# C times the states on GpSimd for 14 of 16 groups, five state buffers, silu in place, the odd heads' k by chunk

## The chip, the cores and the metric

The kernel runs on one core of a Trainium2 chip. A core has a matrix engine (TensorE, PE in the profile), a vector engine (VectorE, DVE), an engine for activation functions (ScalarE, ACT), a programmable engine (GpSimd, POOL) and a queue engine (SyncE, SP) that starts transfers. Each takes its instructions in a fixed order from its own queue, and semaphores hold an instruction back until what it needs is there. The metric is the device time of one execution in microseconds; lower is better.

## The reference

The input x is 16 sequences of 512 tokens with 256 features. Four blocks follow one another, each with a layer norm in front and a residual sum behind it: a state-space block, a gated feed-forward block with 4-bit quantization, a linear attention, and the same feed-forward block again with the same weights.

```python
x = x + mamba(layernorm(x));   x = x + ffn(layernorm(x))
x = x + linattn(layernorm(x)); x = x + ffn(layernorm(x))
# mamba, for every token t: 256 channels d, 16 states n
dA  = dt[t, d] * A[d, n]
h   = exp(dA) * h + (sum_d(dA * u[t, d]) * B[t, n])     # the added term is the same for all d
y   = sum_n(h[d, n] * C[t, n]) + Dp[d] * u[t, d]
# ffn: q() quantizes blocks of 16 to a 4-bit grid times a scale
ffn = q(silu(q(x) @ q(w_gate).T) * (q(x) @ q(w_up).T)) @ q(w_down).T
# linattn: 16 heads of 16, feature map elu + 1 on q and k, causal running sums
y   = (q . cumsum(k v)) / (q . cumsum(k) + 1e-6)
```

## The kernel before

All numbers are fp32, except the rounding operand of the quantizer (bf16). Tiles have 128 partitions.

The state-space block of one sequence (`mamba`) has 256 channels times 16 states, that is 4096 rows of 512 tokens. A tile holds 128 rows (16 states of 8 channels) twice, side by side: a group of 128x1024. There are 16 groups per sequence (`steps`: two halves e, four j, two q0). For each, SyncE spreads the channels' dt over the partitions (`spread`, a transfer from DRAM), ScalarE makes the decays exp(dt A) (`decay`, L466 and L469, into one of two `bars`), VectorE runs the recurrence as a scan along time (L485) into a state buffer `h`, and VectorE multiplies the states by C, in place (L489); C is one row tile `cm` used for both halves. When two groups are done, TensorE adds the rows of a channel with four matmuls into the bank `py` (L495). There are three state buffers (tag "hs"). After the last group of a half, ScalarE copies `py` out (L500).

The feed-forward block (`ffn`) quantizes the normed x (`fp4_steps`: a maximum per block, L212; half and its reciprocal, L217 and L219; the division, L226; on ScalarE the rounding operand, L230; two rounding steps, L232 and L233; the product with the scale, L234). Then, chunk by chunk of 128 tokens and half by half of 704 hidden features, TensorE makes gate and up (L535), ScalarE the tanh of half the gate into `sg` (L541), and VectorE (tanh + 1) times gate (L542) and times half of up (L545) into `h`. The chunk is quantized by the same steps, transposed, and multiplied by the down weights (L574). Names end in _f for the first and in _g for the second feed-forward block.

The attention makes q and k as features by tokens (L607 to L615), multiplies k by a mask that keeps the odd heads (`ko`, one ScalarE instruction on 128x1024 per sequence, L624), and then works by chunk: scores (L653), the causal mask (L660), the values, and the running sum of k v. The denominator is put in shape by a GpSimd copy `dx` (L694) of 128x256, transposed by TensorE (L699) and used on VectorE (L704). `kt` (L710) is the chunk's k by tokens.

The layer norm (`layernorm`) takes statistics on VectorE (L356 to L359), the power -0.5 on GpSimd (`rstd`, 128x4, L361) and normalizes on VectorE (`xn`, L364). The rstd of the four norms and the dx copies are what GpSimd does after the start.

Order: the program is written as generators that yield weights, in units meant as microseconds. `by_turns` always advances the half whose share of its given total is smallest, `weave` alternates pieces of two. For sequence b, first come its state-space block and the beginning of its first feed-forward block, up to a total FIRST, beside the second feed-forward block of sequence b-2 and the norm of the attention of b-1 (FRONT + FFN2); then the rest of that feed-forward block (CHUNKS) beside the attention (ATTN). A group of `mamba` yields 3.5. The compiler's scheduler then orders each engine's queue from this: the earlier written goes first among what it expects to be ready, so engines' orders differ from the written one (two scans can stand next to each other before the first one's multiplication).

```python
FIRST, CHUNKS, FRONT, ATTN, FFN2 = 80.0, 30.0, 7.85, 23.0, 42.0
halves = [(some(new, FIRST), FIRST)]
halves.append((weave(last_ffn(b - 2), some(at, FRONT), 0), FRONT + FFN2))
by_turns(halves)
by_turns([(new, CHUNKS), (at, ATTN if b > 1 else FRONT + ATTN)])
```

Of the kernel before, what the change touches and what calls it, by code (L numbers as in the profile page):

```python
# [10 lines left out]
F32 = mybir.dt.float32  # L11
# [21 lines left out]
def kernel(  # L33
# [411 lines left out]
    def mamba(b, xt):  # L445
# [29 lines left out]
        for at, (e, j, q0) in enumerate(steps):  # L475
            bar = ahead
            if at + NSP - 1 < len(steps):
                sps.append(spread(*steps[at + NSP - 1]))
            if at + 1 < len(steps):
                ahead = decay(sps[at + 1], *steps[at + 1])  # L480
            if j == 0 and q0 == 0:
                py = ps_y.tile([P, S], F32, tag="y", name=f"py_{b}_{e}")
                nc.tensor.matmul(py, d_diag[:, e], u[:, e, :], start=True, stop=False)
            h = one.tile([P, 2, S], F32, tag="hs", name=f"h_{b}_{e}_{j}_{q0}", bufs=3)
            nc.vector.tensor_tensor_scan(  # L485
                h.rearrange("p i t -> p (i t)"), bar.rearrange("p i t -> p (i t)"),
                inp.rearrange("p i t -> p (i t)"), 0.0, ALU.mult, ALU.add,
            )
            nc.vector.tensor_tensor(h, h, cm.unsqueeze(1).to_broadcast([P, 2, S]), ALU.mult)  # L489
            if q0 == 0:  # L490
                h0 = h
            else:

                for q in range(4):
                    nc.tensor.matmul(  # L495
                        py[32 * q : 32 * q + 32, :], red[:, j, :], (h0, h)[q // 2][:, q % 2, :],
                        start=False, stop=(j == 3),
                    )
            if j == 3 and q0 == 2:
                nc.scalar.copy(yT[:, e, :], py)  # L500
            yield 3.5


        for c in range(0, NC, 2):
# [12 lines left out]
    def ffn(i, nm, xt):  # L517
# [8 lines left out]
        def hidden(c):  # L526

            h = act.tile([P, FF], F32, tag="h", name=f"h_{nm}_{c}", bufs=2)
            for f in range(2):
# [3 lines left out]
                for pw, wT in ((pg, wgT), (pu, wuT)):  # L533
# [3 lines left out]
                            start=(k == 0), stop=(k == ND - 1),  # L537
                        )

                sg = act.tile([P, HF], F32, tag="sg", name=f"sg_{nm}_{c}_{f}", bufs=2)  # L540
                nc.scalar.activation(sg, pg[:, :HF], AF.Tanh, scale=0.5)  # L541
                nc.vector.scalar_tensor_tensor(  # L542
                    sg, sg, 1.0, pg[:, :HF], ALU.add, ALU.mult
                )
                nc.vector.scalar_tensor_tensor(  # L545
                    h[:, cols], sg, 0.5, pu[:, :HF], ALU.mult, ALU.mult
                )
                yield 1
            fp4(act, h, FF, f"{nm}_{c}")
            hs.append(h)  # L550
# [42 lines left out]
    def attention(b, xt):  # L593
# [25 lines left out]
            qk.append(ft)  # L619
        qf, kf = qk  # L620


        ko = att.tile([P, ND, S], F32, tag="ko", name=f"ko_{b}", bufs=1)
        nc.scalar.activation(ko, kf, AF.Copy, scale=odd_heads[:, 0:1])  # L624
        yield 0.1

        def scores(c):

            tok = ts(c, P)
# [15 lines left out]
            )  # L645
            yield 0.1

            psc = [bank(f"psc_{b}_{c}_{g}") for g in range(4)]
            for s in range(NH // 4):
                e, odd = divmod(s, 2)  # L650
                for g in range(4):
                    rows = slice(32 * g, 32 * g + (2 * HD if odd else HD))
                    nc.tensor.matmul(  # L653
                        psc[g][:, ts(s, P)], (ko if odd else kf)[rows, e, tok],
                        qf[rows, e, tok], start=True, stop=True,
                    )
            sm = []
# [12 lines left out]
        def attend(c, vp, sm):  # L670
# [19 lines left out]
            num = att.tile([P, ND, P], F32, tag="num", name=f"num_{b}_{c}")  # L690
            nc.scalar.copy(num, pn)

            dx = att.tile([P, ND * HB, HD], F32, tag="dx", name=f"dx_{b}_{c}")
            nc.gpsimd.tensor_copy(  # L694
                dx, den[:, c * NH : (c + 1) * NH].unsqueeze(2).to_broadcast([P, NH, HD])
            )
# [8 lines left out]
            if c < NC - 1:  # L705
                pk = bank(f"pk_{b}_{c}")
                for e in range(ND):
                    nc.tensor.transpose(pk[:, ts(e, P)], kf[:, e, tok], ident)
                kt = att.tile([P, D], F32, tag="kt", name=f"kt_{b}_{c}")
                nc.scalar.copy(kt, pk[:, :D])  # L710
                pkv = bank(f"pkv_{b}_{c}")[:, :D].rearrange("p (e t) -> p e t", t=P)
                if c > 0:
# [82 lines left out]

    FIRST, CHUNKS, FRONT, ATTN, FFN2 = 80.0, 30.0, 7.85, 23.0, 42.0

    def some(gen, total):  # L800

# [74 lines left out]
```

## Time and profile before

| | |
|---|---|
| median of 3 runs | 2910.93 us (2910.67 to 2912.76) |
| the profiled execution's own time | 2910.69 us |
| its span, first to last instruction | 2908.9 us |
| granted TensorE clock, mean | 0.915 |
| scans L485, DVE | 256 of 2277 ns |
| multiplications by C L489, DVE | 256 of 1213 ns |
| rstd L361, POOL | 64; median 1006 to 1912 ns by norm |
| dx copies L694, POOL | 64; median 400 ns |
| ko L624, ACT | 16 of 1149 ns |

A group's line in the profile has its place, engine, operation, operands with shapes, number, then busy time, mean duration of one, and the engine's idle time before them with what ended it. A timeline line has start, length, engine, place and operands. VectorE starts an instruction some 0.08 us before the recorded end of the one in front, so durations add up to slightly more than the busy time. One sequence takes about 173 us in the steady part; the last 275 us, after the last sequence's scans, hold feed-forward and attention alone.

### The profile page before, as it was taken

The numbers are of one execution on the slowest core, as the hardware profiler recorded it, in microseconds if no ns is written. First come the engines' busy times: TensorE is split into PE (matmuls) and PEld (weight loads), VectorE is DVE, ScalarE is ACT, GpSimd is POOL, SyncE is SP. The second block draws the span as 40 slices with busy tenths as digits, with TensorE's granted clock in tenths as the row PEclk, the third lists the DMA queues.
The fourth block names the chain that finished last, engine by engine and source line by source line (L and its number), as shares of the span: only waits on it lengthen the run. The fifth ranks groups of instructions, "written<-read, shape, count | busy, mean of one in ns | idle before, by whom it ended". The sixth has DMA issues, their size and how long they took to land.

```text
span 2908.9 us, 33292 instructions
## 1 busy us (share of the span) xinstructions
PE 2441.2 (84%) x12639; PEld 1428.2 (49%) x12639; DVE 2545.1 (87%) x3795; ACT 1349.0 (46%) x2286; POOL 121.1 (4%) x153
## 2 busy tenths in 40 slices
PE   5676888888888988888888888888888888887887
PEld 2233545454554545455454545545455454545555
DVE  7897889989899898989989898998989999898565
ACT  5555454454545445453545445444544544542122
POOL 2000000000000000000000000000000000000000
PEclk8787899998998999899999999999999899989898
DMA  5332112031321313122031321303122130310000
GB/s 159 87 80 73 51 44 80 15 95 44 80 59 29 81 29 86 53 61 63 21 88 44 80 58 44 80 15 95 44 80 59 36 81 22 84 47 8 1 1 15
DMA packets 64372, 165.21 MB, mean 57 GB/s; under 512 B 8434, under 2 KB 26836, under 8 KB 64212
## 3 DMA queue, kind: packets, MB, share of 16 engines
q1 hardware_dynamic: 62592, 162.03, 21.4%
q8 instruction: 99, 1.62, 0.2%
q10 hardware_dynamic: 1620, 1.06, 0.1%
q14 instruction: 61, 0.50, 0.1%
HBM read 146.28 MB, written 16.78 MB: 56 GB/s over the span
## 4 chain that ended last, share of the span: by engine, by line
DVE 55%; PE 29%; ACT 7%; issue 5%; POOL 2%; POOLq 0%; DVEq 0%; ACTq 0%
DVE h L485 16%; DVE h L489 7%; PE pqk L607 3%; DVE sm L660 2%; PE po_g L574 2%; PE pg_f L535 2%; PE pu_f L535 2%; PE pg_g L535 2%; DVE amax_f L212 2%; PE pu_g L535 2%; PE pz L396 2%; PE py L495 2%; DVE h_f L234 1%; DVE v_f L232 1%; DVE v_f L226 1%
## 5 line engine op out<-in xcount | busy, mean ns | idle before, releaser
L485 DVE TENSOR_TENSOR_SCAN h<-bar,inp 128x1024 f32<-128x1024 f32 x256 | 578.1, 2277 | 10.1 <-ACT inp L441 8.9
L466 ACT ACTIVATE bar<-sp,a_col 128x511 f32<-128x511 f32 x512 | 348.7, 715 | 411.3 <-DVE h L485 410.8
L495 PE MATMUL py<-h,red 128*32 128x512 f32 x1024 | 271.4, 684 | 89.1 <-DVE h L489 89.1
L489 DVE TENSOR_TENSOR h<-h,cm 128x1024 f32<-128x1024 f32 x256 | 309.2, 1213 | 0.0
L469 ACT ACTIVATE bar<-bar 128x1022 f32<-128x1022 f32 x256 | 269.8, 1054 | 4.5
L574 PE MATMUL po_g<-wdT,hqT_g 128*128 128x256 f32 (+1 forms) x768 | 199.8, 403 | 33.1 <-ACT hqT_g L565 33.1
L574 PE MATMUL po_f<-wdT,hqT_f 128*128 128x256 f32 (+1 forms) x768 | 204.7, 410 | 7.8 <-ACT hqT_f L565 7.7
L535 PE MATMUL pg_f<-wgT,tT_f 128*128 128x352 f32 x512 | 200.5, 517 | 2.5 <-DVE sm L660 2.2
L535 PE MATMUL pu_f<-wuT,tT_f 128*128 128x352 f32 x512 | 180.0, 475 | 14.4 <-DVE sm L660 14.4
L574 PEld LDWEIGHTS po_f<-wdT,hqT_f 128*128 128x128 f32 (+1 forms) x768 | 141.4, 197 | 96.3 <-issue 26.8
L574 PEld LDWEIGHTS po_g<-wdT,hqT_g 128*128 128x128 f32 (+1 forms) x768 | 138.3, 193 | 94.3 <-ACT hqT_g L565 47.2
L535 PE MATMUL pg_g<-wgT,tT_g 128*128 128x352 f32 x512 | 178.4, 471 | 0.0
L535 PE MATMUL pu_g<-wuT,tT_g 128*128 128x352 f32 x512 | 173.5, 461 | 0.0
L660 DVE TENSOR_TENSOR sm<-psc,causal 128x512 f32<-128x512 f32 x256 | 163.5, 680 | 9.9 <-PE psc L653 7.9
L230 ACT ACTIVATE big_f<-v_f 128x704 bf16<-128x704 f32 (+1 forms) x80 | 67.3, 841 | 203.2 <-DVE v_f L226 203.0
L535 PEld LDWEIGHTS pu_f<-wuT,tT_f 128*128 128x128 f32 x512 | 100.9, 199 | 79.1 <-DVE sm L660 21.7
L607 PE MATMUL pqk<-tT_a,w_qkv_sb 128*128 128x512 f32 x256 | 135.6, 670 | 0.7 <-ACT tT_a L377 0.7
L535 PEld LDWEIGHTS pg_g<-wgT,tT_g 128*128 128x128 f32 x512 | 97.8, 195 | 74.9 <-issue 37.1
L535 PEld LDWEIGHTS pg_f<-wgT,tT_f 128*128 128x128 f32 x512 | 94.7, 205 | 70.5 <-issue 17.7
L535 PEld LDWEIGHTS pu_g<-wuT,tT_g 128*128 128x128 f32 x512 | 98.1, 192 | 55.1 <-issue 1.5
L495 PEld LDWEIGHTS py<-h,red 128*32 128x32 f32 x1024 | 36.4, 114 | 176.8 <-DVE h L489 118.0
L541 ACT ACTIVATE sg_g<-pg_g 128x352 f32<-128x352 f32 x128 | 58.8, 459 | 108.2 <-PE pg_g L535 108.0
(224 smaller groups left out, 4483.8 us busy)
## 6 DMA issues: line engine op xcount, KB each, us to landing
sp<-dd SPq DMA_DIRECT2D x256, 512.0 KB, 4.6
x<-in_L_attn_a_x_dram SPq DMA_DIRECT2D x16, 512.0 KB, 4.7
dd<-dt SPq DMA_DIRECT2D x128, 64.0 KB, 1.7
out_dram<-x SPq DMA_DIRECT2D x16, 512.0 KB, 3.0
w_qkv_sb<-in_L_attn_b_W_attn_dram ACTq DMA_DIRECT2D x1, 768.0 KB, 6.8
raw_d<-in_L_ffn_w_down_dram SPq DMA_DIRECT2D x1, 704.0 KB
raw_g<-in_L_ffn_w_gate_dram SPq DMA_DIRECT2D x1, 640.0 KB, 6.4
raw_u<-in_L_ffn_w_up_dram SPq DMA_DIRECT2D x1, 640.0 KB, 6.2
```

Source lines behind the costliest of these rows:

```text
L212: nc.vector.tensor_reduce(amax, src.rearrange("p (b k) -> p b k", k=BLK), AX.X, ALU.max, apply_absolute_value=True,)
L230: nc.scalar.activation(big, v, AF.Abs, scale=STEP)
L466: nc.scalar.activation(bar[:, i, 1:S], sp[:, i, 1:S], AF.Exp, scale=a_col[:, g : g + 1])
L469: nc.scalar.activation(bar[:, :, 1:S], bar[:, :, 1:S], AF.Square)
L485: nc.vector.tensor_tensor_scan(h.rearrange("p i t -> p (i t)"), bar.rearrange("p i t -> p (i t)"), inp.rearrange("p i t -> p (i t)"), 0.0, ...
L489: nc.vector.tensor_tensor(h, h, cm.unsqueeze(1).to_broadcast([P, 2, S]), ALU.mult)
L495: nc.tensor.matmul(py[32 * q : 32 * q + 32, :], red[:, j, :], (h0, h)[q // 2][:, q % 2, :], start=False, stop=(j == 3),)
L535: nc.tensor.matmul(pw[:, :HF], xqT[:, k, ts(c, P)], wT[:, k, cols], start=(k == 0), stop=(k == ND - 1),)
L541: nc.scalar.activation(sg, pg[:, :HF], AF.Tanh, scale=0.5)
L574: nc.tensor.matmul(po[:, :D], hqT[:rows, r, :], wdT[:rows, r, :], start=(r == 0), stop=(r == NR - 1),)
L607: nc.tensor.matmul(pz, w_qkv_sb[:, k, ts(je, P)], xnT[:, k, :], start=(k == 0), stop=(k == ND - 1),)
L660: nc.vector.tensor_tensor(t, psc[g].rearrange("p (s t) -> p s t", t=P), causal.unsqueeze(1).to_broadcast([P, NH // 4, P]), ALU.mult,)
```

## The change

The multiplication of the states by C moves from VectorE to GpSimd for the groups 0 to 13 of each sequence; groups 14 and 15 keep VectorE. There are five state buffers instead of three. In the feed-forward block the tanh is written straight into the hidden tile `h`, and both products are made there in place; the tiles `sg` go. `ko` is made per chunk (128x256, two buffers) inside `scores`, instead of once per sequence (128x1024). `dx` and `kt` have one buffer instead of two. The weights of the interleaving are changed: 2.3 instead of 3.5 for a group, FIRST 61 instead of 80, FRONT 7.8 instead of 7.85, and the yield behind the old `ko` goes.

```diff
-            h = one.tile([P, 2, S], F32, tag="hs", name=f"h_{b}_{e}_{j}_{q0}", bufs=3)
+            h = one.tile([P, 2, S], F32, tag="hs", name=f"h_{b}_{e}_{j}_{q0}", bufs=5)
...
-            nc.vector.tensor_tensor(h, h, cm.unsqueeze(1).to_broadcast([P, 2, S]), ALU.mult)
+            by = nc.vector if at >= len(steps) - 2 else nc.gpsimd
+            by.tensor_tensor(h, h, cm.unsqueeze(1).to_broadcast([P, 2, S]), ALU.mult)
...
-            yield 3.5
+            yield 2.3
...
-                sg = act.tile([P, HF], F32, tag="sg", name=f"sg_{nm}_{c}_{f}", bufs=2)
-                nc.scalar.activation(sg, pg[:, :HF], AF.Tanh, scale=0.5)
-                nc.vector.scalar_tensor_tensor(
-                    sg, sg, 1.0, pg[:, :HF], ALU.add, ALU.mult
-                )
-                nc.vector.scalar_tensor_tensor(
-                    h[:, cols], sg, 0.5, pu[:, :HF], ALU.mult, ALU.mult
-                )
+                hc = h[:, cols]
+                nc.scalar.activation(hc, pg[:, :HF], AF.Tanh, scale=0.5)
+                nc.vector.scalar_tensor_tensor(hc, hc, 1.0, pg[:, :HF], ALU.add, ALU.mult)
+                nc.vector.scalar_tensor_tensor(hc, hc, 0.5, pu[:, :HF], ALU.mult, ALU.mult)
...
-        ko = att.tile([P, ND, S], F32, tag="ko", name=f"ko_{b}", bufs=1)
-        nc.scalar.activation(ko, kf, AF.Copy, scale=odd_heads[:, 0:1])
-        yield 0.1
...
+            ko = att.tile([P, ND, P], F32, tag="ko", name=f"ko_{b}_{c}")
+            nc.scalar.activation(ko, kf[:, :, tok], AF.Copy, scale=odd_heads[:, 0:1])
...
-                        psc[g][:, ts(s, P)], (ko if odd else kf)[rows, e, tok],
+                        psc[g][:, ts(s, P)], ko[rows, e, :] if odd else kf[rows, e, tok],
...
-            dx = att.tile([P, ND * HB, HD], F32, tag="dx", name=f"dx_{b}_{c}")
+            dx = att.tile([P, ND * HB, HD], F32, tag="dx", name=f"dx_{b}_{c}", bufs=1)
...
-                kt = att.tile([P, D], F32, tag="kt", name=f"kt_{b}_{c}")
+                kt = att.tile([P, D], F32, tag="kt", name=f"kt_{b}_{c}", bufs=1)
...
-    FIRST, CHUNKS, FRONT, ATTN, FFN2 = 80.0, 30.0, 7.85, 23.0, 42.0
+    FIRST, CHUNKS, FRONT, ATTN, FFN2 = 61.0, 30.0, 7.8, 23.0, 42.0
```

## The prediction

> **What bounds the kernel now.** I read first the page's busy table and its chain, then the groups of instructions, then windows of one sequence, then the few places where GpSimd and VectorE already work at the same time.
>
> ```profile
> span 2908.9 us, 33292 instructions
> PE 2441.2 (84%) x12639; PEld 1428.2 (49%) x12639; DVE 2545.1 (87%) x3795; ACT 1349.0 (46%) x2286; POOL 121.1 (4%) x153
> DVE 55%; PE 29%; ACT 7%; issue 5%; POOL 2%; POOLq 0%; DVEq 0%; ACTq 0%
> L485 DVE TENSOR_TENSOR_SCAN h<-bar,inp 128x1024 f32<-128x1024 f32 x256 | 578.1, 2277 | 10.1 <-ACT inp L441 8.9
> L489 DVE TENSOR_TENSOR h<-h,cm 128x1024 f32<-128x1024 f32 x256 | 309.2, 1213 | 0.0
> 953.10:1082.00 128.90, 111.52 (x666) 66.65 (x664) 121.72 (x176) 60.24 (x104) 5.46 (x7) 0.93 0.20 54
> 1082.00:1126.00 44.00, 37.88 (x123) 20.84 (x123) 34.88 (x60) 22.91 (x37) 1.01 (x1) 0.92 0.29 72
> ```
>
> VectorE (DVE) is the fullest engine and carries 55% of the chain; TensorE (PE) is close behind with 29%. GpSimd (POOL) is almost empty. The two window lines (window, length, then busy us of PE, PEld, DVE, ACT, POOL, then clock, DMA share, GB/s) split one period of about 173 us: in the first 129 us lie all 16 scans of a sequence, and DVE is busy for 121.7 of them, PE for 111.5.
>
> Does POOL work run freely beside DVE? The next lines are from the views of lines L694 and L361 (min/median/max) and the timelines of DVE and POOL.
>
> ```profile
> L694 POOL COPY dx<-den x64: 396/400/2394, 288.2 to 2816.3; 128x256 f32<-128x256 f32 x64
> L361 POOL TENSOR_TENSOR rstd_a<-var_a,neg_half x16: 1006/1912/1913, 221.3 to 2756.4; 128x4 f32<-128x4 f32 x16
> ...
> 288.64 2.48 DVE L485 TENSOR_TENSOR_SCAN h<-bar,inp 128x1024 f32<-128x1024 f32 x1
> 288.19 3.12 POOL L694 COPY dx<-den 128x256 f32<-128x256 f32 x2 [59.18 <-DVE den L760]
> 2699.59 1.10 DVE L226 TENSOR_TENSOR v_f<-h_f,inv_f 128x704 f32<-128x704 f32 x1
> 2699.22 0.74 POOL L694 COPY dx<-den 128x256 f32<-128x256 f32 x2 [51.10 <-DVE half_f L217]
> 876.44 1.22 DVE L232 SCALAR_TENSOR_TENSOR v_g<-big_g,v_g 128x1024 f32<-128x1024 bf16 x1
> 876.62 1.91 POOL L361 TENSOR_TENSOR rstd_a<-var_a,neg_half 128x4 f32<-128x4 f32 x1 [8.78 <-DVE var_a L359]
> ```
>
> It does not. Two copies that need 0.40 each took 3.12 around a scan, the second ending at 291.31, 0.19 after the scan (291.12). The scan took 2.48 instead of 2.28, and the multiplication at 2699.59 took 1.10 instead of its mean 0.89, so POOL holds DVE up too. The rstd at 876.62 took 1.91 instead of 1.01: it ends 0.87 after L232. All these DVE instructions read two tensors from SBUF. Beside L542 and L545, which read one from SBUF and one from PSUM, the copy keeps its 0.40. So I call "exclusive" a DVE instruction with two SBUF tensors: the scans L485, the multiplication L489, the quantizer's L226, L232, L233, L234, and L615, L747, L416, L430, L750. One of those and a reading POOL instruction run one after the other. The rest ("free": L212, L542, L545, L660, L356, L364, L578 and so on) overlaps with POOL.
>
> The Trainium skill states the same in SBUF — State Buffer, Who interferes with whom: a VectorE instruction with two SBUF inputs and a GpSimd instruction that reads SBUF block each other for a whole instruction, and whichever starts first wins. It speaks against this change more strongly than the sum below: with no cover at all, every moved multiplication would cost DVE its whole length, and the time would go up.
>
> **The change part by part.**
>
> Removed from DVE: 14 x 16 = 224 of the L489 multiplications. One lasts 1.213 and the next starts 0.08 before its end (835.00 + 1.21 against 836.13), so each frees 1.13: **-254 us** of DVE.
>
> Added to POOL: 224 multiplications of 128x1024 by a broadcast row. No row has one. Lower bound: one element per step at the slope of the memsets, (524 - 204) ns / (512 - 128) = 0.83 ns, so 0.95 us with start. Upper bound: the whole 0.40 of a 256-element copy for each quarter and each of two inputs, 3.2 us. (The pow at 5437 ns for 32 elements is another kind of operation.) Nearest: what a copy adds to an exclusive DVE instruction, 0.20 to 0.21 for 256 elements of one input; eight times that is 1.6 to 1.7, and with the copy's remaining 0.2 about 1.8 to 1.9. A second stream through the same port may cost some more: I take **2.0 us**. POOL is then busy 28 us of a 173 us period, far from a bound itself.
>
> The Trainium skill, GPSIMD Engine Reference, Elementwise — side-by-side cycle accounting, gives 4497 ns for a two-input add of 2048 elements, which I estimate as 2.25 us here. By that figure the stall below would be 1.05 instead of 0.90, 236 us in total, and the sum -8 instead of -43: no gain worth the name. No run here shows it yet.
>
> The stall on DVE. For each of the 224 scans I went along DVE's recorded order behind it, without the L489s; an exclusive instruction at the head is let through first (77 of 224 cases: POOL waits for it), and then free instructions and idle time are added up to the next exclusive one. That is what POOL can hide behind. At 2.0 us a mean of 1.10 is hidden and 0.90 stalls: **+201 us**. At 0.95 it is 0.31 (70 us), at 1.75 0.74 (167), at 2.6 1.27 (285), at 3.2 1.65 (370). Break-even is at 2.3. In all, DVE's timeline of the 129 us window adds up to 44.6 us of free work and 7.2 us idle against 28 us of POOL, so the cover exists; it only lies badly.
>
> POOL's queue: the multiplications now stand in front of rstd (L361, four per sequence, three of them in the scan window) and dx (L694). xn (L364) on DVE waits for rstd, already 44 us in all. POOL is taken 28/129 = 22% of the window, for 1.0 more on average: 48 x 0.22 x 1.0 = **+10 us**; at the worst 48 x 2.0 = 96. dx feeds transposes of PE whose product L704 is read on DVE; one POOL length late is hidden by PE's other work, else 0.22 x 64 x 1.0 = 14.
>
> PE's matmuls L495 now wait for POOL. A pair of groups is ready 2 to 5 us later, and PE's in-order queue waits with it (L495 waited 89 us for L489 so far). Five state buffers instead of three let two more scans run on meanwhile; scans are some 8 us apart on average, so I count nothing; without that cover 2 us for each of 112 pairs, 224.
>
> Yields 3.5 to 2.3, FIRST 80 to 61, FRONT 7.85 to 7.8: the scan groups keep 36.8/61 = 60% of the first part's weight instead of 56/80 = 70%. The other half of that part, 49.85 units, then advances by 1.88 units per group instead of 2.18: about a seventh less work between scans. Taken as nothing, since the hidden 1.10 is mostly bounded by the next exclusive instruction; at the worst a seventh of it, 0.16 x 224 = 35.
>
> Silu in place: the same three instructions, so no work changes. tanh on ACT now waits for the readers (transposes, L561) of the h buffer two chunks back, where L545 waited for them before, and the decays L466 and L469 stand behind it on ACT. L545's whole idle time is 19 us, mostly for PE's pu; that is also the bound. Taken 0.
>
> ko by chunk: 64 copies of 128x256 by the like row L691 (364 ns), 23.3 us, for 18.4 us in 16 (L624): +5 us on ACT, which is 46% busy; 0, at worst 5. kt and dx with one buffer: kt waits for the pkv matmuls of the chunk before, a whole chunk earlier: 0. dx waits for the transposes of the chunk before, in POOL's queue, with multiplications behind it (a rival below).
>
> Sum on DVE: -254 + 201 + 10 = -43. DVE carries 55% of the chain and PE, at 111.5 of 128.9 us in the window, does not get shorter; I let 0.6 of a DVE gain reach the end: -25. The profiled execution took 2910.69 (1.8 outside its span), the median is 2910.93, so the two are one number: **2885 us**. Under 0.2% (6 us) nothing can be told from no change.
>
> **The rivals.**
>
> A, the forecast: half of a POOL multiplication hides. With stalls of 0.7 to 1.0 (157 to 224 us) the sum is -87 to -20, of which 0.6 arrives: 2859 to 2899.
>
> B, the port decides against it: the instruction behind a scan is exclusive more often, or POOL takes more than 2.3. For it: 77 cases already begin so, and two scans often stand back to back (L485 x2). If only 0.55 of 2.0 hides, the stall is 1.45 x 224 = 325 and the sum -254 + 325 + 10 = +81: 2992. Against it: the 44.6 us of free work. It decides from a stall of 1.09 per multiplication on, and a DVE loss goes to the end undiminished.
>
> C, cover is good: POOL at 1.6 or free work moved behind the scans. Stall 0.31, 70 us: -174, of which 0.6 arrives: 2806. PE's 111.5 of 128.9 is the floor, about 17 us per period.
>
> D, POOL's queue: dx already waits for PE's transposes 157.6 us in 32 cases, 4.9 each. With one buffer multiplications stand behind that; if half of it reaches the scans, 79 us more than the forecast: about 2964. Against it: five state buffers and that most of these waits are early arrivals.
>
> E, the freed DVE time becomes waiting for PE, or stall equals saving: within 6 us of 2911.
>
> **How the numbers follow.** A 0.37, C 0.15, E 0.08, B 0.33, D 0.07. Faster by over 0.2%: 0.52; within: 0.08; slower: 0.40. The 80% range goes from C's 2806, rounded down, to just short of B's 2992: 2800 to 2985. A alone has 2859 to 2899.
>
> **What would show it.** L489 on POOL with a spacing of about 2.0 when undisturbed; durations of the scans and of L226 to L234 raised by 0.9 x 224 = 201 us altogether, while L542, L545, L660 and L212 stay as they are; DVE busy by the page about 2545 - 254 + 201 = 2490; idle before xn up by 10; L495 waiting for POOL instead of DVE. The forecast is wrong if POOL needs over 2.3, if exclusive instructions gather behind the scans, or if idle before L364 or L495 grows by tens of us.

## The result and the profile after

The changed kernel takes **3144.44 us** (median; 3143.98 to 3145.93) against 2911.04 us for the kernel before on the same chip: a ratio of **1.080** with a 95% interval of 1.078 to 1.082. It is 233 us slower. The forecast was 2885 with a range up to 2985, so the time lies outside the range, on the side of rival B (the port decides) and well beyond the price of that rival. The profiled execution took 3145.93 us, 1.7 more than its span.

The page of the kernel after, with the lines that answer to those shown of before (busy time of each engine, shares of the chain, the groups of C times the states and of the scans, the dx copies):

```profile
span 3144.2 us, 33577 instructions
PE 2510.8 (80%) x12639; PEld 1477.6 (47%) x12639; DVE 2550.9 (81%) x3571; ACT 1358.4 (43%) x2334; POOL 794.0 (25%) x377
DVE 48%; PE 26%; issue 7%; POOL 6%; ACT 5%; DMA 1%; SPq 0%; POOLq 0%; ACTq 0%; DVEq 0%
L491 POOL TENSOR_TENSOR h<-h,cm 128x1024 f32<-128x1024 f32 x224 | 661.4, 2961 | 1159.0 <-DVE h L485 1098.7
L485 DVE TENSOR_TENSOR_SCAN h<-bar,inp 128x1024 f32<-128x1024 f32 x256 | 722.1, 2835 | 54.3 <-ACT bar L469 41.3
L690 POOL COPY dx<-den 128x256 f32<-128x256 f32 x64 | 36.4, 568 | 381.1 <-PE pr L695 199.5
```

VectorE has 224 instructions fewer (3795 to 3571) and is busy for 2550.9 us, where it was busy for 2545.1. So 254 us of multiplications went away, and the busy time is still 6 us up because other instructions became longer: the scans alone grew from 578.1 to 722.1 us. Worse, nearly the whole loss of time stands outside the busy time: span minus busy is 593 us on VectorE, and was 364. TensorE shows the like, 2510.8 of 3144.2 us busy against 2441.2 of 2908.9; it has the same 12639 matmuls, at a lower granted clock (0.864 instead of 0.915). Neither engine was given more work; both wait more.

The view of windows, one period of the steady part (window, length, busy us of PE, PEld, DVE, ACT, POOL, TensorE's clock, DMA share, GB/s): the first line from the first scan of a sequence to the end of its last, the second the rest.

```profile
1031.80:1144.20 112.40, 89.06 (x558) 52.47 (x556) 97.42 (x119) 46.65 (x79) 43.52 (x19) 0.83 0.24 62
1144.20:1219.50 75.30, 64.70 (x231) 38.50 (x231) 59.14 (x104) 37.29 (x65) 4.00 (x3) 0.93 0.16 40
```

The period grew from 172.9 to 187.7 us. The scans now lie closer together, in 112 us instead of 129, but the rest of the period grew from 44 to 75 us: work that used to stand between the scans has been pushed behind them. In the scan window VectorE is busy for 87% of the time (94% before) and TensorE is granted 0.83 of its clock (0.93 before).

By "the port" is meant below whatever makes a GpSimd instruction that reads SBUF and a VectorE instruction such as a scan wait for each other. How it is shared is seen in the timelines of VectorE and GpSimd in that window (start, length, engine, place, operands, and in brackets the idle time in front).

```profile
1092.56 1.73 DVE L217 TENSOR_SCALAR half_f<-amax_f 128x44 f32<-128x44 f32 x1
1106.03 4.42 DVE L485 TENSOR_TENSOR_SCAN h<-bar,inp 128x1024 f32<-128x1024 f32 x1
1112.23 2.90 DVE L485 TENSOR_TENSOR_SCAN h<-bar,inp 128x1024 f32<-128x1024 f32 x1 [1.71 <-ACT bar L469]
1115.82 3.98 DVE L485 TENSOR_TENSOR_SCAN h<-bar,inp 128x1024 f32<-128x1024 f32 x1
...
1091.89 2.35 POOL L491 TENSOR_TENSOR h<-h,cm 128x1024 f32<-128x1024 f32 x1 [2.30 <-DVE h L485]
1105.94 2.36 POOL L491 TENSOR_TENSOR h<-h,cm 128x1024 f32<-128x1024 f32 x1 [11.35 <-DVE h L485]
1110.62 2.37 POOL L491 TENSOR_TENSOR h<-h,cm 128x1024 f32<-128x1024 f32 x1 [2.32 <-DVE mv_g L357]
1115.30 2.35 POOL L491 TENSOR_TENSOR h<-h,cm 128x1024 f32<-128x1024 f32 x1 [2.31 <-DVE h L485]
1119.94 2.36 POOL L491 TENSOR_TENSOR h<-h,cm 128x1024 f32<-128x1024 f32 x1 [2.30 <-DVE h L485]
```

The multiplication that starts on GpSimd at 1105.94 ends at 1108.30. The scan that starts 0.09 us after it ends at 1110.45, that is 2.15 after the multiplication: it waited and then took its own time, and shows 4.42 us instead of 2.28. Only then does GpSimd get its next turn (1110.62), so multiplications follow each other every 4.6 to 4.7 us. The stalled scan has a second effect. There are two buffers of decays, and a scan that ends late frees its one late: by the chain of waits ScalarE starts on the next one at 1110.53, 0.08 after the scan's end, and the scan at 1112.23 stands idle for 1.71 us until that `bar` is there. And the small L217 at 1092.56, a tensor_scalar that needs 0.18 us alone, ends 0.05 us after GpSimd's multiplication (1094.24) and takes 1.73.

The waits of VectorE, summed over the span (what it waited for, us in total, times, longest), the kernel after:

```profile
DVE qk L613 <- ACT ep L612: 138.7, 30, 6.8
DVE x L576 <- PE po_g L572: 77.7, 19, 6.2
DVE x L734 <- PE pro L730: 51.9, 34, 3.0
DVE h L485 <- ACT bar L469: 41.3, 29, 10.2
DVE xn_m L364 <- POOL rstd_m L361: 35.3, 13, 2.9
```

Before, the same five stood at 25, 16, 28, under 2 and 12.5 us; three of them as the view of before has them:

```profile
DVE qk L615 <- ACT ep L614: 25.3, 29, 1.6
DVE x L578 <- PE po_g L574: 16.1, 6, 6.2
DVE xn_m L364 <- POOL rstd_m L361: 12.5, 13, 1.0
```

None of them alone explains the 229 us of added idle time; the experiments have to say which part of the change brings which.

### The profile page after: what moved, and what is told of

Read it like the earlier page. It is cut to its first block, busy times and chain, and to the rows that moved or that the text cites. A ratio compares the mean times of both kernels' runs of the same rounds, so it can differ in the third digit from the quotient of the medians.

```text
span 3144.2 us, 33577 instructions
## 1 busy us (share of the span) xinstructions
PE 2510.8 (80%) x12639; PEld 1477.6 (47%) x12639; DVE 2550.9 (81%) x3571; ACT 1358.4 (43%) x2334; POOL 794.0 (25%) x377
## 4 chain that ended last, share of the span: by engine, by line
DVE 48%; PE 26%; issue 7%; POOL 6%; ACT 5%; DMA 1%; SPq 0%; POOLq 0%; ACTq 0%; DVEq 0%
DVE h L485 14%; POOL h L491 4%; PE py L497 3%; PE po_g L572 3%; PE pu_f L537 2%; PE pqk L605 2%; PE pg_f L537 2%; DVE v_g L232 2%; DVE sm L656 2%; DVE amax_f L212 2%; DVE amax_g L212 2%; DVE v_g L226 2%; DVE half_f L217 2%; DVE v_f L226 1%; DVE v_g L233 1%
## 5 line engine op out<-in xcount | busy, mean ns | idle before, releaser
L491 POOL TENSOR_TENSOR h<-h,cm 128x1024 f32<-128x1024 f32 x224 | 661.4, 2961 | 1159.0 <-DVE h L485 1098.7
L485 DVE TENSOR_TENSOR_SCAN h<-bar,inp 128x1024 f32<-128x1024 f32 x256 | 722.1, 2835 | 54.3 <-ACT bar L469 41.3
L537 PE MATMUL pg_f<-wgT,tT_f 128*128 128x352 f32 x512 | 215.5, 550 | 68.1 <-DVE sm L656 34.3
L572 PE MATMUL po_g<-wdT,hqT_g 128*128 128x256 f32 (+1 forms) x768 | 221.9, 437 | 46.5 <-ACT hqT_g L563 46.5
L537 PE MATMUL pu_f<-wuT,tT_f 128*128 128x352 f32 x512 | 199.3, 517 | 30.1 <-DVE sm L656 30.1
L572 PEld LDWEIGHTS po_g<-wdT,hqT_g 128*128 128x128 f32 (+1 forms) x768 | 154.1, 214 | 124.2 <-ACT hqT_g L563 60.5
L656 DVE TENSOR_TENSOR sm<-psc,causal 128x512 f32<-128x512 f32 x256 | 162.3, 676 | 20.1 <-PE pn L680 10.9
L361 POOL TENSOR_TENSOR rstd_f<-var_f,neg_half 128x4 f32<-128x4 f32 x16 | 16.1, 1007 | 577.9 <-DVE var_f L359 577.9
L537 PEld LDWEIGHTS pu_f<-wuT,tT_f 128*128 128x128 f32 x512 | 110.5, 219 | 106.3 <-DVE sm L656 43.2
L613 DVE SCALAR_TENSOR_TENSOR qk<-ep 128x512 f32<-128x512 f32 x64 | 46.2, 721 | 138.7 <-ACT ep L612 138.7
L690 POOL COPY dx<-den 128x256 f32<-128x256 f32 x64 | 36.4, 568 | 381.1 <-PE pr L695 199.5
```

Of the source, the lines that this page charges most:

```text
L485: nc.vector.tensor_tensor_scan(h.rearrange("p i t -> p (i t)"), bar.rearrange("p i t -> p (i t)"), inp.rearrange("p i t -> p (i t)"), 0.0, ...
L491: by.tensor_tensor(h, h, cm.unsqueeze(1).to_broadcast([P, 2, S]), ALU.mult)
L537: nc.tensor.matmul(pw[:, :HF], xqT[:, k, ts(c, P)], wT[:, k, cols], start=(k == 0), stop=(k == ND - 1),)
L572: nc.tensor.matmul(po[:, :D], hqT[:rows, r, :], wdT[:rows, r, :], start=(r == 0), stop=(r == NR - 1),)
L656: nc.vector.tensor_tensor(t, psc[g].rearrange("p (s t) -> p s t", t=P), causal.unsqueeze(1).to_broadcast([P, NH // 4, P]), ALU.mult,)
```

## The experiments

**Stall** below is the time by which VectorE's instructions last longer than the median of their form in the kernel before, summed where the excess is over 0.05 us; it is 1 us before and **248 us** after. "Idle" is the span minus VectorE's busy time. The kernel before runs at 2911 to 2913 us beside all of these. Each expectation names the theories as they stood when it was written.

### All of the change but GpSimd, and GpSimd alone

e1: the change with every multiplication on VectorE.

```diff
-            by = nc.vector if at >= len(steps) - 2 else nc.gpsimd
+            by = nc.vector
```

> The changed kernel with all 16 multiplications by C back on VectorE; five state buffers, silu in place, ko by chunk, single dx and kt and the new weights stay. Theory 1 (port: a GpSimd multiplication and a VectorE instruction that reads two SBUF tensors exclude each other, 2.36 us each time) and theory 2 (lateness: what costs is that C times h comes later, and TensorE waits) both expect the loss to go: 2880 to 2940 us, scans back at 2.28 us each, half-clock time of TensorE back near 499 us. Theory 3 (weights: the new weights 2.3, 61 and 7.8 bunch the scans and leave VectorE without work later) expects at least half of the loss of 233 us to stay: over 3030 us. Theory 4 (the small edits: one dx buffer, one kt buffer, tanh into h) expects over 3030 us as well.

e2: the kernel before with these two lines alone changed (three buffers, old weights, no other edit).

```diff
-            nc.vector.tensor_tensor(h, h, cm.unsqueeze(1).to_broadcast([P, 2, S]), ALU.mult)
+            by = nc.vector if at >= len(steps) - 2 else nc.gpsimd
+            by.tensor_tensor(h, h, cm.unsqueeze(1).to_broadcast([P, 2, S]), ALU.mult)
```

> The kernel before with nothing changed but the multiplication by C on GpSimd for groups 0 to 13: three state buffers, old weights, old silu, ko, dx and kt. Theories 1 and 2 expect the whole loss or more, since three buffers give less room: 3100 to 3250 us. Theories 3 and 4 expect less than a third of it: under 2990 us.

Measured: e1 2975.35 us, ratio 1.022 [1.020, 1.023]; e2 3187.58, ratio 1.094 [1.093, 1.096]. e2 has a stall of 279 us and an idle time of 600. So the move to GpSimd is by itself a loss larger than the whole change, and the rest of the change is a loss too, of 64 us, which the forecast had at nothing. From e1 to the full change are 169 us: VectorE's busy time grows by 25 (2526 to 2551) and its idle time by 144 (449 to 593). In the waits of e1 the places that GpSimd lengthens can be told from those that were long without it:

```profile
DVE x L576 <- PE po_g L572: 20.6, 6, 6.2
DVE xn_m L364 <- POOL rstd_m L361: 11.6, 13, 0.9
```

With GpSimd these two are 77.7 and 35.3 us (the wait before the like `po_f` falls, from 48.6 to 20.2), and the wait for the decays goes from nothing to 41.3; the largest one, before `qk`, is 132.8 us in e1 already.

### The weights

e3: the change with the old weights. e5: the kernel before with the new ones. e6: e1 with the old ones.

```diff
-            yield 2.3
+            yield 3.5
...
-    FIRST, CHUNKS, FRONT, ATTN, FFN2 = 61.0, 30.0, 7.8, 23.0, 42.0
+    FIRST, CHUNKS, FRONT, ATTN, FFN2 = 80.0, 30.0, 7.85, 23.0, 42.0
```

> The changed kernel with the old weights: 3.5 per group, FIRST 80, FRONT 7.85. Theories 1, 2 and 4 expect 3090 to 3200 us, as the change itself (3144). Theory 3 expects under 3000 us and the idle time of VectorE before L613 (qk, 139 us) back near 25.

> The kernel before with the new weights alone (2.3 per group, FIRST 61, FRONT 7.8). Asks where the 63 us come from that the change costs with all multiplications on VectorE (2975 against 2912). Weights theory: 2950 to 2990 us. Edits theory (one dx and kt buffer, tanh into h, five state buffers): 2905 to 2930 us.

> The small edits and the five state buffers with the old weights, all multiplications on VectorE. Weights theory: 2900 to 2930 us. Edits theory: 2950 to 2990 us and the idle time of VectorE before L613 (qk) near 130 us as in the run with all but the multiplication.

Measured: e3 3147.44 (1.081), e5 2897.51 (0.995 [0.994, 0.997]), e6 2980.16 (1.023). The weights are worth between -14 and -3 us wherever they are exchanged. In e3 the stall is 197 us and VectorE is busy for 2507 us, 44 less than in the full change, and yet the time is the same: its idle time is 640 us. That GpSimd's work is in the way because of the weights is out.

### The number of state buffers

e9: e1 with three state buffers. e15: the full change with three.

```diff
-            h = one.tile([P, 2, S], F32, tag="hs", name=f"h_{b}_{e}_{j}_{q0}", bufs=5)
+            h = one.tile([P, 2, S], F32, tag="hs", name=f"h_{b}_{e}_{j}_{q0}", bufs=3)
```

> All multiplications on VectorE, new weights, all small edits, but three state buffers again. Asks which part of the rest costs the 63 us (2975 against 2912). If the five state buffers do it, by letting the scans run ahead and leaving VectorE without filling work before L613 later: 2890 to 2920 us and idle before L613 under 60 us. If the small edits do it (single dx and kt, tanh into h, ko by chunk): 2960 to 2990 us, idle before L613 over 110 us.

> The changed kernel with three state buffers. Port theory, with the buffers adding their own 96 us as on VectorE: 3030 to 3070 us. If the loss of the port and that of the buffers share one cause (scans run ahead and later work has no cover), or three buffers are too few for the slower multiplication (the version with GpSimd alone had 3188): 3120 to 3220 us.

Measured: e9 2878.99 us, ratio 0.988 [0.987, 0.990]; e15 3123.22, ratio 1.073 [1.071, 1.074]. More buffers make this kernel slower. The busy times and VectorE's waits, first of e1 (five buffers), then of e9 (three):

```profile
PE 2479.1 (83%) x12639; PEld 1458.8 (49%) x12639; DVE 2525.8 (85%) x3795; ACT 1361.0 (46%) x2334; POOL 164.7 (6%) x153
DVE qk L613 <- ACT ep L612: 132.8, 30, 6.8
DVE x L576 <- PE po_f L572: 48.6, 16, 4.6
```

```profile
PE 2421.3 (84%) x12639; PEld 1431.8 (50%) x12639; DVE 2545.6 (89%) x3795; ACT 1358.5 (47%) x2334; POOL 124.6 (4%) x153
DVE qk L613 <- ACT ep L612: 28.9, 16, 2.5
DVE x L576 <- PE po_g L572: 27.3, 32, 6.2
```

VectorE does the same work, but with five buffers the scans of a sequence gather in 113 us, as in the kernel after (130 us in e9), and the feed-forward steps and projections between them come later; VectorE then stands before `qk` for 133 us instead of 29. The gathering alone does not decide, though: in e10 and e8 below, with five buffers too, the scans of a sequence lie in 113 and 112 us, and the wait before `qk` is 78 and 21 us. So the 233 us of the change are, put on in this order: weights and small edits with three buffers -32 (2911 to 2879), five buffers +96 (to 2975), GpSimd +169 (to 3144). In the other order GpSimd is +244 (2879 to 3123) and the buffers +21: they share part of their cost, and neither figure is theirs alone.

### The port, or C times the states being late

e4 keeps GpSimd as long, on the same semaphores, but lets it read nothing from SBUF: three memsets of the state buffer (0.95, 0.95 and 0.53 us) stand in place of the multiplication. It leaves out the multiplication by C for the groups 0 to 13.

```diff
-            by = nc.vector if at >= len(steps) - 2 else nc.gpsimd
-            by.tensor_tensor(h, h, cm.unsqueeze(1).to_broadcast([P, 2, S]), ALU.mult)
+            if at >= len(steps) - 2:
+                nc.vector.tensor_tensor(h, h, cm.unsqueeze(1).to_broadcast([P, 2, S]), ALU.mult)
+            else:
+                nc.gpsimd.memset(h, 0.25)
+                nc.gpsimd.memset(h, 0.5)
+                nc.gpsimd.memset(h[:, 0, :], 0.25)
```

> The changed kernel with each GpSimd multiplication by C replaced by memsets of the state buffer on GpSimd, 1024 + 1024 + 512 elements, by the rows of the memsets about 0.95 + 0.95 + 0.52 = 2.4 us, nearly the length of the multiplication (2.36 us): the same lateness for TensorE, but GpSimd reads nothing from SBUF. It leaves the multiplication by C out for groups 0 to 13. Theory 1 expects scans at 2.28 us, and the time at 2930 us or below, since 254 us of VectorE work are gone and no stall replaces them. Theory 2 expects that TensorE waits as in the changed kernel and the time stays over 3050 us.

Measured: 2780.88 us, ratio 0.955 [0.953, 0.956]. From the page and the groups of e4:

```profile
PE 2369.6 (85%) x12639; PEld 1420.6 (51%) x12639; DVE 2309.0 (83%) x3571; ACT 1357.4 (49%) x2334; POOL 676.5 (24%) x825
L485 DVE TENSOR_TENSOR_SCAN h<-bar,inp 128x1024 f32<-128x1024 f32 x256 | 581.0, 2279 | 38.9 <-ACT bar L469 24.3 <-ACT inp L441 9.8 <-POOL h L495 2.0
L493 POOL MEMSET h<- 128x1024 f32 x224 | 213.6, 953 | 901.6 <-DVE h L485 820.6 <-PE pqk L609 26.6 <-PE pu_f L541 26.5
```

The scans are back at 2279 ns and the stall is 15 us. Of the 365 us between the spans of the full change and of e4, 242 are VectorE's busy time (2551 to 2309) and 123 its idle time (593 to 470). So it is the reading from SBUF that costs. A hand-over to GpSimd of about the same length without the reading takes 194 us off e1, where VectorE is relieved by 217 (2526 to 2309): the idle time stays nearly as it was (449 to 470).

### The scan taken off the port

e7: the full change, but the scan's added term lies in PSUM, one row tile for both halves (one of the seven PSUM buffers is given up for it, and a copy on ScalarE falls away); the scan becomes two of 512. Then a scan reads one tensor from SBUF and one from PSUM. e8: the same on e1, with all multiplications on VectorE.

```diff
+        inp_b = inp
+        inp = ps_i.tile([P, S], F32, tag="inp", name=f"inpp_{b}")
+        nc.vector.tensor_tensor(inp, inp_b[:, 0, :], pg, ALU.mult)
...
+            for i in range(2):
+                nc.vector.tensor_tensor_scan(
+                    h[:, i, :], bar[:, i, :], inp, 0.0, ALU.mult, ALU.add
+                )
```

> The changed kernel with the scan's added term in PSUM (one bank, so six banks are left for the rest; two scans of 512 per group, since the two halves share it, some 0.16 us more per group, 41 us in all). A scan then reads one SBUF tensor. Port theory: scans no longer grow beside GpSimd (2 x 1.22 to 2 x 1.30 us), stalls fall from 248 to under 110 us (the quantizer's steps and the two-input rest), and against its control with the multiplications on VectorE it is faster, by 40 to 190 us, where the change itself was slower by 169. If something else than the port stalls the scan (memory bandwidth, the in-place write), scans still grow and it stays slower than its control by over 100 us.

> The control: the same kernel with the scan's added term in PSUM, all multiplications on VectorE. All theories: 2975 plus some 41 us for the second scan of a group, plus up to 60 for the missing PSUM bank: 2990 to 3080 us.

Measured: e7 2845.86 us, ratio 0.977 [0.976, 0.979]; e8 2808.34, ratio **0.964** [0.963, 0.966], the fastest of all whole computations here. Busy times, groups and the wait before `qk`, of e7 and then of e8:

```profile
PE 2400.7 (84%) x12639; PEld 1427.5 (50%) x12639; DVE 2371.4 (83%) x3827; ACT 1351.6 (48%) x2318; POOL 651.9 (23%) x377
L488 DVE TENSOR_TENSOR_SCAN h<-bar,inpp 128x512 f32<-128x512 f32 x512 | 600.9, 1200 | 25.0 <-ACT bar L471 14.4
L493 POOL TENSOR_TENSOR h<-h,cm 128x1024 f32<-128x1024 f32 x224 | 531.4, 2378 | 1083.6 <-DVE h L488 919.7
DVE qk L615 <- ACT ep L614: 137.9, 30, 6.7
```

```profile
PE 2425.6 (86%) x12639; PEld 1412.9 (50%) x12639; DVE 2539.3 (90%) x4051; ACT 1370.5 (49%) x2318; POOL 117.6 (4%) x153
L488 DVE TENSOR_TENSOR_SCAN h<-bar,inpp 128x512 f32<-128x512 f32 x512 | 606.8, 1201 | 0.7 <-issue 0.2
DVE qk L615 <- ACT ep L614: 21.1, 15, 4.4
```

With scans that need one SBUF operand, GpSimd and VectorE run side by side: the scans keep 1200 ns, the multiplication on GpSimd has a mean of 2378 instead of 2961, and the stall falls from 248 to 70 us. What GpSimd costs falls from 169 to 38 us. That is the port shown a second time, from the other end. But it is still no gain: the 40 to 190 us that the expectation gave to GpSimd over its control did not come, and the control itself, expected at 2990 to 3080 us, was far faster than that. Here VectorE is truly relieved, by 168 us (2539 to 2371), and the end does not follow: its idle time grows by 206 us (268 to 474), 117 of them before `qk` (21 to 138). So the same relief that reached the end to nine tenths from e1 to e4 is worth less than nothing from e8, whose idle time was small. In e4 and e7 the idle time comes out at 470 and 474 us, whatever it was without GpSimd.

### Where the 167 us of e8 come from

Against e1, e8 splits the scan and moves its operand. e10: e1 with the scan split, both operands in SBUF. e11: the kernel before with the new weights and e8's edit, nothing else. e13: e8 with three buffers.

```diff
-            nc.vector.tensor_tensor_scan(
-                h.rearrange("p i t -> p (i t)"), bar.rearrange("p i t -> p (i t)"),
-                inp.rearrange("p i t -> p (i t)"), 0.0, ALU.mult, ALU.add,
-            )
+            for i in range(2):
+                nc.vector.tensor_tensor_scan(
+                    h[:, i, :], bar[:, i, :], inp[:, i, :], 0.0, ALU.mult, ALU.add
+                )
```

> All multiplications on VectorE, new weights, small edits, five state buffers, seven banks, and each group's scan as two scans of 512 from SBUF. Asks why the run with the added term in PSUM and the multiplications on VectorE fell to 2808 us with the same VectorE work as 2975. If the split scans (and the order that follows from them) do it: under 2880 us. If the place of the added term does it: 2975 to 3030 us.

> The kernel before with the new weights (2898 us alone) and the added term in PSUM with split scans, but three state buffers and none of the small edits: 2780 to 2860 us if the gain of the PSUM version (167 us against its counterpart) is its own, 2880 to 2940 if it only undid what the five buffers and the edits had cost.

> Everything that was good so far together: multiplications on VectorE, three state buffers, new weights, small edits, the added term in PSUM with split scans. If the loss by five buffers (96 us from SBUF) holds here as well: 2700 to 2790 us against 2808 with five. If the PSUM version has already removed it: 2795 to 2830.

Measured: e10 2894.18 us (0.994 [0.992, 0.995]), e11 2829.2 (0.971 [0.970, 0.973]), e13 2825.88 (0.971 [0.969, 0.973]). The split alone takes 81 us off e1; the place in PSUM, with the copy on ScalarE that falls away and one bank less for the rest, another 86. The group of scans in e10:

```profile
L486 DVE TENSOR_TENSOR_SCAN h<-bar,inp 128x512 f32<-128x512 f32 x512 | 610.4, 1208 | 5.1 <-ACT inp L441 3.9 <-ACT bar L469 0.8
```

The scans of e8 last as long (1201 ns), and two of them are longer than one of 1024 (2279). VectorE's busy time is 2526, 2545 and 2539 us in e1, e10 and e8; its idle time is 449, 348 and 268. So none of the gain is work saved on VectorE; it is time in which it waits. TensorE is also busy for less, 2479, 2418 and 2426 us, at a clock of 0.893, 0.914 and 0.923. With the term in PSUM, five buffers are no longer worse than three (2808 against 2826). Whether the order of the queues, TensorE's clock or both decide is not settled by these runs, and of the 86 us for the place of the operand the cause stays open.

### Half of the multiplications

e12: GpSimd for every second group, 7 of 16. e16: GpSimd for the first seven groups in a row.

```diff
-            by = nc.vector if at >= len(steps) - 2 else nc.gpsimd
+            by = nc.gpsimd if q0 == 0 and at < len(steps) - 2 else nc.vector
...
+            by = nc.vector if at >= 7 else nc.gpsimd
```

> The changed kernel with GpSimd for the first group of each pair only (7 of 16), the second on VectorE. Port theory: each moved multiplication costs about the same, so half of the 169 us against the counterpart with all on VectorE: 3030 to 3090 us, stalls 100 to 150 us. If the cost came from GpSimd being too slow for a row of scans (queueing), 7 of 16 would cost next to nothing: 2960 to 2995 us.

> GpSimd for the first seven groups of a sequence in a row, VectorE for the other nine: as many moved as in the version with every other group (2999). Row theory (it costs most when scans and multiplications alternate group after group, 4.65 us each, with nothing else let through): 3040 to 3080 us. If only the number moved counts: 2985 to 3015 us.

Measured: e12 2998.98 us (1.030 [1.028, 1.031]), e16 3000.78 (1.031 [1.029, 1.032]). Half of the multiplications cost 24 or 25 us above e1, not half of 169. After e12 I held that consecutive multiplications are what hurts, since GpSimd and the scans then take strict turns; e16 puts seven in a row and costs the same, so that theory fell. Stalls are 110 and 106 us for 127 saved, a somewhat smaller part than in the full change (248 of 254). What grows faster than their number is not the stall but the idle time: 449 us with none, 470 and 480 with seven, 593 with fourteen.

### GpSimd's queue

e14: the full change with rstd and dx taken out of GpSimd's queue: rstd as a reciprocal on VectorE (its square root is left out), dx copied by ScalarE. e17: the same on e1, as its control.

```diff
-        nc.gpsimd.tensor_tensor(rstd, var, neg_half, ALU.pow)
+        nc.vector.reciprocal(rstd, var)
...
-            nc.gpsimd.tensor_copy(
+            nc.scalar.copy(
```

> The changed kernel with GpSimd left to the multiplications: the power -0.5 of the norm becomes a reciprocal on VectorE (the square root is left out) and the dx copy goes to ScalarE. Queue theory (part of the 144 us of extra idle time on VectorE comes from rstd and dx standing behind multiplications on GpSimd): 3030 to 3095 us, that is over 50 us below 3144; idle before xn gone. Otherwise: 3100 to 3160 us.

> The control of the run with the queue freed: rstd as a reciprocal on VectorE (square root left out), dx on ScalarE, and all multiplications on VectorE. Queue theory: taking rstd and dx off an otherwise empty GpSimd is worth little, 2930 to 2970 us against 2975, so that most of the 125 us are the queue's. If the gain is that of a quicker rstd in any version: 2840 to 2900 us.

Measured: e14 3019.15 us (1.037 [1.035, 1.038]), e17 2902.84 (0.998 [0.996, 0.999]). The edit takes 125 us off the full change, but 72 off e1, where nothing stands in GpSimd's queue. The difference, **53 us**, is what rstd and dx lose by standing behind multiplications, if the two effects simply add (the runs of e14 and e17 scatter by 10 and 12 us). What is left of GpSimd's cost, 3019 - 2903 = 116 us, comes with a stall (243 us) that is about equal to the multiplications removed. VectorE's busy time is 2540 against 2529 us; the idle time grows from 377 to 476. The busy times of e14, then of e17 (span 3016.1 and 2906.4 us):

```profile
PE 2467.4 (82%) x12639; PEld 1471.1 (49%) x12639; DVE 2539.9 (84%) x3635; ACT 1377.0 (46%) x2398; POOL 662.7 (22%) x249
PE 2453.0 (84%) x12639; PEld 1426.6 (49%) x12639; DVE 2529.2 (87%) x3859; ACT 1386.4 (48%) x2398; POOL 14.9 (1%) x25
```

One more thing differs between these runs: TensorE's granted clock. Its mean is 0.923 in e8, 0.917 in e17, 0.893 in e1 and e14, and 0.864 in the kernel after. The clock records of the trace know only full and half speed here; the time at half is 432, 480, 637, 644 and 855 us of the span. In these five it falls as VectorE's idle time grows, but e4 and e7, idle for 470 and 474 us, have the highest clocks of all, 0.933 and 0.929. Whether the low clock lengthens the waits or the waits of TensorE lower the clock, none of the runs tells apart. TensorE's busy time gives an idea of how much could lie in it: 2511 us in the kernel after against 2479 in e1 and 2441 before, 32 of the 169 us and 70 of the 233, if all of it were on the path (the ends of matmuls are modelled in the profile, so this is an estimate).

## Why the prediction was wrong

**The port's rule: right, but too narrow.** VectorE instructions with two SBUF tensors and reading GpSimd instructions take turns; e4 and e7 show it by taking the reads away at either end. Those with one PSUM operand (L544, L545, L656) stayed at 515, 514 and 676 ns, as said. What the rule missed, the tensor_scalars, stands under the stall.

**GpSimd's price: mis-sized.** Taken 2.0 us, within bounds of 0.95 to 3.2. The view of L491 (min/median/max) has

```profile
L491 POOL TENSOR_TENSOR h<-h,cm x224: 2333/2365/4442, 52.8 to 2812.0; 128x1024 f32<-128x1024 f32 x112
```

so 2.33 at the least and 2.37 in the median. The Trainium skill's GPSIMD Engine Reference, Elementwise — side-by-side cycle accounting, from which 2.25 had been estimated, was nearer than my sum from the copies; the trace has some 0.1 more than that estimate. With 2.25 the forecast's sum would have been -8 us and rival E, still far from what came.

**The stall: near, and partly by luck.** 201 us were forecast, 248 measured. The walk along VectorE's order had its break-even, a stall of 244 beside the 10 for the queue, at a price of 2.3; the price came out just above that and the stall at 248. That this fits so well is luck: the walk did not know that VectorE's order would change, and the instructions called free were not all free. Two rows of before, then three of after:

```profile
L217 DVE TENSOR_SCALAR half_f<-amax_f 128x44 f32<-128x44 f32 (+1 forms) x80 | 14.5, 182 | 1.1
L359 DVE TENSOR_SCALAR var_m<-mv_m 128x4 f32<-128x4 f32 x16 | 2.5, 159 | 0.0
...
L217 DVE TENSOR_SCALAR half_f<-amax_f 128x44 f32<-128x44 f32 (+1 forms) x80 | 57.1, 714 | 2.0
L359 DVE TENSOR_SCALAR var_m<-mv_m 128x4 f32<-128x4 f32 x16 | 16.5, 1029 | 0.5
L212 DVE TENSOR_REDUCE amax_f<-h_f 128x44 f32<-128x704 f32 x64 | 55.5, 867 | 0.6
```

The tensor_scalars L217 and L359 read one tensor and yet stood still beside GpSimd: 14.5 and 2.5 us became 57.1 and 16.5, with those of other names some 60 of the 248 us. The reduction L212 is unchanged (56.4 to 55.5). The whole trace of after bears this out: of VectorE's instructions that start inside one of the 144 multiplications shorter than 2.45 us, at least 0.3 us before its end, all 71 scans, both L226 and all 29 tensor_scalars (L217, L359 and one L364, which the prediction had named as free) are held for 0.6 us or more. None of the 87 others, which are reductions, statistics, reciprocals and instructions with one operand in PSUM, is longer by more than 0.03 us. Of the 248 us, 143 are on the scans and 25 on the 32 multiplications by C that VectorE keeps. The Trainium skill, SBUF — State Buffer, Who interferes with whom, lists tensor_scalar among the operations that can enter a mode on both port pairs and says that a reduction can't on this chip; I had taken only its sentence on two inputs. The trace agrees with it, by the 1.73 us shown above.

**"Sum on DVE ... I let 0.6 of a DVE gain reach the end": the step that failed.** The end was forecast from VectorE's sum alone. The measured sum is -254 + 248, about nothing, and VectorE is busy for 6 us more than before. By the forecast's own rule that is rival E, no change. The kernel lost 233 us all the same, 229 of it as idle time. The sum counts how long VectorE works and not when; e3 with 44 us less work on VectorE takes as long as the full change. The waits that grew are before the decays (41 us before L485; e4, without stalled scans, has 24 of these, so not all come from late scans), before xn_m, since GpSimd's queue holds up rstd (12.5 to 35.3 us), and before TensorE's products (`po_g`, 16 to 78). That the fixed queues of VectorE and TensorE then wait for each other is my reading of these waits; no run shows it by itself. Nor was there a fixed share like my 0.6 for a gain: it is 0.9 from e1 to e4 and below nothing from e8 to e7.

**"Five state buffers ... I count nothing": the second step that failed.** +96 us without GpSimd, +21 with it. The prediction had 224 us beside this term, for L495 without its cover, but that is another reason, and the range did not hold it. With five buffers the scans gather; why the kernel is slower for it is not shown, since e8 has them as close together and is 167 us faster than e1.

**GpSimd's queue: mis-sized.** +10 us taken, 96 named as the worst; 53 measured. (The 44 us that xn was said to wait for rstd before are 40 by the view of waits; 4 of them are waits for TensorE.)

**Weights, silu in place, ko, kt, dx: small, as said,** though with the other sign than the worst cases. The weights are -14 us in the kernel before, all of this together -32. (L545's idle time before was said to be mostly for pu; it is 9 of 19 us.)

**The rivals.** B named the side and the mechanism, and its price of 2992 came from a stall of 325 us; the stall was 248, just past its turning point of 1.09 per multiplication (248/224 = 1.11). So B holds as a mechanism, and fails as a sum: the loss is not in stalls beyond what was saved. C is out. Of E the condition came true, stall equals saving, and the time did not. D, a price of 79 us for GpSimd's queue, was nearer in kind than its chance of 0.07 said: the queue costs 53, though the runs don't part dx from rstd. The single buffer of dx can't be what the loss needs: e2 keeps two and loses 276 us.

**What stays open.** Of GpSimd's 169 us on top of e1, 53 are its queue. The other 116 come with the port, since without the reading there is no loss (e4); some 100 of them are idle time on VectorE (377 to 476 us from e17 to e14). How much of this is lost order and how much TensorE's clock is not settled, and neither is why five buffers cost 96 us without GpSimd and 21 with it.

## What to carry to other kernels

Before work is moved from VectorE to GpSimd, count what on VectorE reads a second tensor from SBUF or is a tensor_scalar: beside such work the move took from VectorE about as much as it gave, here 248 of 254 us, and it made a longer queue on GpSimd besides. A sum over one engine's busy time was no forecast here, where two engines are busy for 80% or more and run fixed queues: with VectorE's work equal to within 1% (2526 to 2551 us in e1, e8 and the kernel after), the times lie between 2808 and 3144 us, almost wholly by idle time. Here it paid to put one operand of the scan in PSUM and to leave the work where it was (e11 against e5: 2897.5 to 2829.2 us), and more buffers had to be tried, not assumed to be free.

## What was not expected of the hardware

- A scan with one operand in PSUM costs no more than one from SBUF: 1201 against 1208 ns for 128x512.
- Not every GpSimd instruction that reads SBUF holds VectorE up for its whole length. In the kernel before, the power for rstd started at 1097.35 and took 1.01 us; the multiplication below started 0.16 later, in the midst of it, and kept its 0.89, as in 12 more such cases:

```profile
1097.35 1.01 POOL L361 TENSOR_TENSOR rstd_f<-var_f,neg_half 128x4 f32<-128x4 f32 x1 [46.04 <-DVE var_f L359]
1097.51 0.89 DVE L234 TENSOR_TENSOR h_g<-v_g,half_g 128x704 f32<-128x704 f32 x1
```

  The page of the Trainium skill named above speaks of the pair being held for the whole instruction. That fits the multiplication (the scan at 1106.03 ended 2.15 after it, so it can have begun its own 2.28 only 0.13 before the multiplication's end), and not this power of 128x4; there the measurement decides. Nor do the short copies hold a tensor_scalar there: 12 L364 of the kernel before start 0.14 us after a `dx` copy of 0.40 and keep their 0.40.
- Where both engines have such work ready, they alternate one for one: multiplications every 4.6 to 4.7 us in the stretch shown above, with the scans between them.
